# The row of means by way of DRAM instead of a TensorE transpose

## The chip, the cores and the metric

The kernel runs on one core of a Trainium2 chip, as one launch. The metric is device time in microseconds (us), the median of several executions. Times inside an execution come from one profiled execution and count from the start of its span. The engines are called by their names or as the profile abbreviates them: TensorE (PE, and PEld for its weight loads), VectorE (DVE), ScalarE (ACT), GpSimd (POOL) and SyncE (SP). An engine's name with a q (SPq, ACTq) stands for its instruction queue, where DMA issues are recorded.

## The reference

One transformer block on x of shape (4, 512, 512): four sequences of 512 tokens, 512 features, in float32. Cut to what is computed:

```python
def attn(x):                                  # x is layer-normalised
    q  = (x @ W_q.T).reshape(B, S, 16, 32)
    kv = (x @ W_kv.T).reshape(B, S, 16, 32)
    qf, kvf = fft(q), fft(kv)                 # over the 32 features of a head
    qf, kvf = qf / norm(qf), kvf / norm(kvf)
    kvf = cumsum(kvf, axis=1)                 # over the tokens of a sequence
    v = ifft(qf * kvf).real.reshape(B, S, D)
    return v @ W_o.T

def ffn(x):                                   # weights rounded to fp8 e4m3
    gate = silu((x @ q8(gate_w)) * gate_scale)
    up = (x @ q8(up_w)) * up_scale
    return ((gate * up) @ q8(down_w)) * down_scale

x = x + attn(layernorm(x))
x = x + ffn(layernorm(x))
```

The layer normalisation subtracts each token's mean over its features and divides by its deviation.

## The kernel before, in words

The work on attention is cut into 16 chunks of 128 tokens (four sequences of four chunks). A chunk is held twice: as x (tokens on the partitions, 128 x 512) and as xT (features on the partitions, four blocks of 128 x 128, tokens along the row). The Fourier transform is folded into the weights at the start, so one group of four matmuls makes the spectrum of a chunk (`spectrum`, L358: `pq`, with j = 1 for the keys and values and j = 0 for the queries).

The normalisation is split. The division by the deviation comes after the matmul, as a factor for each token. The subtraction of the mean comes before it, on xT. There the tokens lie along the row, so the means are needed as a row of 128 numbers that is the same on every partition. ScalarE makes the column of negated means, one number for each partition, in two operations (`x_mean`, L287 and L288, tile `less`). `x_row` (L344 to L346) then spreads the column over 128 columns by a broadcast access and lets TensorE transpose it into a PSUM tile `row`, whose every partition holds the row. `x_center` (L348 to L350) adds that row to the four blocks of xT on VectorE. `x_deviation` (L295 to L297) makes the reciprocal deviation on ScalarE and GpSimd.

The order of the instructions is written out by hand. After a prologue that treats chunks 0 to 2, a loop runs i from 3 to 15; its body is called a round here, and work on several chunks is interleaved in it. On each engine the instructions run in the order written. In a round:

- SyncE's queue issues the loads of xT and x for chunk i + 2, the reload of a finished chunk of the first sequence in some rounds (`load_y`, tile `ys`), the store of the attention's result for chunk i - 4 (`finish`, L466, `y_all`), loads of raw feed-forward weights (`load_unit`, L202, `rawf`), the store of the product of spectra for chunk i - 2 (`v_out`, L443, `qv_all`) and its reload in four pieces with another layout (`v_back`, L315, `zv`). In rounds 10 to 14 the same is done for the second normalisation of the first sequence (`y_out`, L491, `xn_all`; `y_back`, L315, `z`).
- TensorE runs the spectrum of chunk i (j = 1), the transpose of the means of chunk i + 1, the spectrum (j = 0), the running sum over tokens of chunk i - 1 (`running`, L413, `cum`) and the projection of chunk i - 3 (`project`, L457, `po`).
- VectorE scales by the norms (`kn`, `qn`, L382), adds the carried sum of the chunk before to the first row (L396), splits into high and low parts (`kl`, L404), finishes a chunk (L465), turns 32 x 32 blocks (`v_turn`, L320: `qvT` from `zv`; `t` from `z`), quantises the feed-forward weights, sums squares (L374), centres xT of chunk i + 1 (L350) and multiplies the spectra (L430, L431).
- ScalarE copies the high part (`kh`, L399), squares the spectra (L369), takes part in the quantisation (L217, L218), copies the last row of the running sum (`carry`, L420) and issues that row's move to partition 0 as a DMA from its own queue (L421, `end`, in twelve of the sixteen chunks), takes the mean of chunk i + 2 (L287, L288), and in rounds 9 to 12 the statistics of the second normalisation.

xT has three buffers, x seven. The PSUM tiles `row` share a tag of two buffers (`tp`) with some tiles outside the loop. The constant tile `tab` holds four 128 x 128 tables; the first (`fwd`, `tab[:, 0, :]`) is read only while the weights are folded in the prologue, the second is the identity that the transposes use.

A DMA tells its end by a semaphore. In the built program there are eight for the DMAs of both queues; they are taken in turn, and a DMA waits for the end of the one that had its semaphore before.

After the loop the feed-forward part runs 48 steps (four sequences of twelve blocks of 128 hidden features): gate and up projections (`gu`, L525), activation on ScalarE (L536), product on VectorE (L539), a split into high and low parts (L550, L552) and the down projection (`pd`, L572). Its first twelve steps overlap with the last chunks of the attention and with the rest of the quantisation.

Of the kernel before, what the change touches and what calls it, by code (L numbers as in the profile page):

```python
# [7 lines left out]
F32 = mybir.dt.float32  # L8
# [7 lines left out]
P = 128  # L16
# [19 lines left out]
def tile_fft_attention_then_fp8_ffn(  # L36
# [38 lines left out]
    nc = tc.nc  # L75
# [13 lines left out]
    dram = ctx.enter_context(tc.tile_pool(name="dram", bufs=1, space=bass.MemoryType.DRAM))  # L89
# [4 lines left out]
    N = len(chunks)  # L94


    tab = const.tile([P, 4, P], F32, name="tab")
# [16 lines left out]
    def big_tile(name, dtype=F32):  # L114
        return big.tile([P, KC, D], dtype, tag="big", name=name)

    raw = []
    for i, w in enumerate((w_kv, w_q, w_oT)):
        t = big_tile(f"raw{i}")
# [31 lines left out]
    wd = const.tile([P, MC, D], F32R, name="wd")  # L151
    y_all = dram.tile([B, TC, P, D], F32, name="y_all")
    xn_all = dram.tile([B, TC, P, D], F32, name="xn_all")
    qv_all = dram.tile([N, P, D], F32, name="qv_all")


# [37 lines left out]
    def load_unit(u):  # L194

        _, src, n, k = units[u]
        staged[u] = big_tile("rawf") if k == 0 else staged[u - 1]
        if src is down_w:
            rows = src[n * KC * P : (n + 1) * KC * P, :]
        else:  # L200
            rows = src[:, n * D : (n + 1) * D]
        nc.sync.dma_start(  # L202
            staged[u][:, k : k + QH, :],
            rows.rearrange("(k p) n -> p k n", p=P)[:, k : k + QH, :],
        )
# [63 lines left out]
    def next_parts(n, in_rounds=False):  # L269

        for f, u in parts[:n]:
            if f is quant_step:
                f(u, in_rounds)
                if in_rounds and u + 2 < U1 and u != 1:
                    wanted.append(u + 2)
            else:
                f(u)
            if f is quant_add and u + 1 < len(units):
                quant_abs(u + 1)
        del parts[:n]  # L280


    def mean(src, name):

        less = work.tile([P, 1], F32, tag="less", name=f"less_{name}", bufs=8)
        each = work.tile([P, D], F32, tag="each", name=f"each_{name}", bufs=1)
        nc.scalar.activation(each, src, AF.Identity, accum_out=less)  # L287
        nc.scalar.activation(less, less, AF.Copy, scale=-1.0 / D)  # L288
        return less
# [32 lines left out]
    def heads(t):  # L322
# [3 lines left out]
    st_x, lesses, rows, xns, pqs, sss, rns, qns, kns, carries, cums, qvs, zs, qvTs, pos = (  # L326
        {} for _ in range(15)
    )

    def nm(i):  # L330
        return "%d_%d" % chunks[i]

    def x_mean(i):
        st_x[i] = lesses[i] = mean(xt[i], nm(i))
# [9 lines left out]
    def x_row(i):  # L344
        rows[i] = ps.tile([P, KC, P], F32, tag="tp", name=f"row_{nm(i)}")
        nc.tensor.transpose(rows[i][:, 0, :], lesses[i].to_broadcast([P, P]), ident)  # L346

    def x_center(i):  # L348
        row = rows.pop(i)[:, 0:1, :].to_broadcast([P, KC, P])
        nc.vector.tensor_tensor(xTs[i], xTs[i], row, ALU.add)  # L350

    def spectrum(i, j):
        if j == 1:
            pqs[i] = {}
        pq = ps.tile([P, D], F32, tag="acc", name=f"pq{j}_{nm(i)}", bufs=4)
        w = (wq, wkv)[j]
        for k in range(KC):
            nc.tensor.matmul(  # L358
                pq, lhsT=xTs[i][:, k, :], rhs=w[:, k, :], start=k == 0, stop=k == KC - 1
            )  # L360
        pqs[i][j] = pq
# [5 lines left out]
    def squared(i, j):  # L367
        sq = sss[i, j] = work.tile([P, D], F32, tag="tmp", name=f"sq{j}_{nm(i)}")
        nc.scalar.activation(sq, pqs[i][j], AF.Square, scale=st_x[i][1])  # L369

    def summed(i, j):
        sq = sss[i, j]
        ss = work.tile([P, H], F32, tag=f"ss{j}", name=f"ss{j}_{nm(i)}")
        nc.vector.tensor_reduce(ss, heads(sq), AX.X, ALU.add)  # L374
        sss[i, j] = ss

    def norms(i, j):
        rns[i, j] = work.tile([P, H], F32, tag=f"rn{j}", name=f"rn{j}_{nm(i)}")
        nc.gpsimd.tensor_tensor(rns[i, j], sss.pop((i, j)), nhalf, ALU.pow)  # L379
# [11 lines left out]
    def k_scaled(i):  # L391
        kn = work.tile([P, D], F32, tag="kn", name=f"kn_{nm(i)}", bufs=1)
        scaled(i, 1, kn)
        if i in carries:
            row = carries.pop(i)
            nc.vector.tensor_tensor(kn[:1, :], kn[:1, :], row, ALU.add)  # L396
        kh = work.tile([P, D], F32R, tag="kh", name=f"kh_{nm(i)}", bufs=3)
        kl = work.tile([P, D], F32R, tag="kl", name=f"kl_{nm(i)}", bufs=3)
        nc.scalar.copy(kh, kn)  # L399
        kns[i] = (kn, kh, kl)  # L400

    def k_low(i):
        kn, kh, kl = kns[i]
        nc.vector.tensor_tensor(kl, kn, kh.bitcast(F32), ALU.subtract)  # L404

    def q_scaled(i):
        qns[i] = work.tile([P, D], F32, tag="qn", name=f"qn_{nm(i)}")
        scaled(i, 0, qns[i])

    def running(i, tag="b"):  # L410
        cum = ps.tile([P, D], F32, tag=tag, name=f"cum_{nm(i)}")
        for n, v in enumerate(kns[i][1:]):
            nc.tensor.matmul(cum, lhsT=tri_r, rhs=v, start=n == 0, stop=n == 1)  # L413
        cums[i] = cum
# [27 lines left out]
    def v_out(i):  # L442
        nc.sync.dma_start(qv_all[i], qvs.pop(i)[0])  # L443

    def v_back(i):
        zs[i] = work.tile([P, KC, P], F32, tag="z", name=f"zv_{nm(i)}")
        blocks(zs[i], qv_all[i])

    def v_turn(i):
        qvTs[i] = work.tile([P, KC, P], F32, tag="qvT", name=f"qvT_{nm(i)}", bufs=1)  # L450
        turned(qvTs[i], zs.pop(i))
# [19 lines left out]
    def load_y(b, chunks=None):  # L471
        if b not in ys:
            ys[b] = big_tile(f"ys_{b}")
        for c in range(TC) if chunks is None else chunks:
            nc.sync.dma_start(ys[b][:, c, :], y_all[b, c])

    def y_stats(b, c):
        st_y[b, c] = stats(ys[b][:, c, :], f"f{b}_{c}")
# [8 lines left out]
    def y_norm(b, c):  # L487
        xns["y", b, c] = normed(ys[b][:, c, :], st_y.pop((b, c)), f"f{b}_{c}")

    def y_out(b, c):  # L490
        nc.sync.dma_start(xn_all[b, c], xns.pop(("y", b, c)))  # L491

    def y_back(b, c):
        if b == 0:
            z = work.tile([P, KC, P], F32, tag="xn", name=f"z_{b}_{c}")
        else:
            z = work.tile([P, KC, P], F32, tag="x", name=f"z_{b}_{c}", bufs=XB)
        blocks(z, xn_all[b, c])
        xns["z", b, c] = z

    def y_turn(b, c):
        if c == 0:
            yhs[b] = big_tile(f"yh_{b}", F32R)
            yls[b] = big_tile(f"yl_{b}", F32R)
        z = xns.pop(("z", b, c))
        t = work.tile([P, KC, P], F32, tag="t", name=f"t_{b}_{c}", bufs=1)
        turned(t, z)
        s = slice(c * P, (c + 1) * P)
        hi, lo = yhs[b][:, :, s], yls[b][:, :, s]
        nc.scalar.copy(hi, t)  # L510
        return lo, t, hi.bitcast(F32)
# [76 lines left out]
    def at(f, i, *more):  # L588
        if 0 <= i < N:
            f(i, *more)  # L590
# [37 lines left out]
    squares(0, 1)  # L628
    norms(0, 1)
    x_row(1)  # L630
    x_center(1)
    spectrum(0, 0)
# [67 lines left out]
    for i in range(3, N):  # L700

        at(load_xT, i + 2)
        at(load_x, i + 2)
        if 0 <= i - (N - 9) < TC:
            load_y(0, [i - (N - 9)])
        spectrum(i, 1)
        k_scaled(i - 1)
        at(finish, i - 4)
        while wanted:
            load_unit(wanted.pop(0))  # L710
        v_out(i - 2)
        c = i - (N - 6)
        if 0 <= c < TC:
            y_norm(0, c)
            y_out(0, c)
        if 0 < c <= TC:
            y_back(0, c - 1)
        v_back(i - 2)
        k_low(i - 1)
        v_turn(i - 3)  # L720
        low = y_turn(0, c - 2) if 1 < c <= TC + 1 else None
        at(x_row, i + 1)
        squared(i, 1)
        at(x_deviation, i + 1)
        next_parts(given[i] // 3, True)
        q_scaled(i - 1)
        if low:
            nc.vector.tensor_tensor(*low, ALU.subtract)
        summed(i, 1)
        norms(i, 1)  # L730
        spectrum(i, 0)
        next_parts((given[i] + 1) // 3, True)
        running(i - 1)
        squared(i, 0)
        carry(i - 1)
        at(x_mean, i + 2)
        at(x_center, i + 1)
        products(i - 1)
        combined(i - 1)
        if 0 <= i - (N - 7) < TC:  # L740
            y_stats(0, i - (N - 7))
        summed(i, 0)
        norms(i, 0)
        next_parts((given[i] + 2) // 3, True)
        project(i - 3)
# [155 lines left out]
```

## Time and profile before

| | us |
|---|---|
| median of 3 runs | 459.96 |
| lowest, highest | 458.78, 460.82 |
| the profiled execution | 459.09 |
| its span | 457.3 |

What the span is made of, by the profile's chain of the work that ended last: the start with the folding of weights up to 16.7 us, the attention's chunks up to some 188 us, the feed-forward part to the end. In the loop a round takes 10.88 us (spectra of successive rounds begin at 114.94, 125.82, 136.71 and 147.58 us). The granted TensorE clock is full in every slice.

How to read the lines that follow: a line of a timeline has the start, the length, the engine, the line of the kernel, the operation, and what is written from what is read; in brackets stands how long the engine was idle before it, and which instruction ended that. A line of the waits has the engine and line that waited, what it waited for, the total, how often, and the longest. Median times from a DMA's issue to its landing, from the page:

| DMA | KB | us to landing |
|---|---|---|
| x, xT loads | 256 | 3.3, 3.2 |
| qv_all store, y_all store, xn_all store | 256 | 4.1, 2.7, 2.3 |
| zv reload, z reload (each of four) | 64 | 2.6, 2.7 |
| rawf load | 512 | 4.7 to 5.3 |
| end (carry), ScalarE's queue | 2 | 2.1 |

### The profile page before, as it was taken

Reading aid. Unit: us, or ns where it says so; the run is one execution under the profiler, and the core shown is the slowest. Engines: PE = TensorE matmul, PEld = TensorE weight load, DVE = VectorE, ACT = ScalarE, POOL = GpSimd, SP = SyncE. Lnnn points to the kernel's source line nnn. Section 1 sums busy time; section 2 is a strip of 40 time slices with the busy share of each in tenths; the row PEclk is TensorE's granted clock in tenths of the full one; section 3 lists DMA queues with packets and bytes.
Section 4 is the critical chain, followed back from the end, with each engine's and each line's share of the span. In section 5 each row is a group of like instructions: output and inputs, shape, how many; then the busy total and the mean of one; then the engine's idle time right before and its main releaser. Section 6 shows DMA issues by size and latency. Waiting matters only on the chain.

```text
span 457.3 us, 5096 instructions
## 1 busy us (share of the span) xinstructions
PE 451.2 (99%) x1692; PEld 309.0 (68%) x1692; DVE 283.1 (62%) x394; ACT 212.8 (47%) x430; POOL 186.1 (41%) x132
## 2 busy tenths in 40 slices
PE   8999999999999999999999999999999999999996
PEld 7544444444444445677888888888888888888885
DVE  1376998997999889797996432343533333522245
ACT  4467665555876632357834225433235432222230
POOL 0377898888797778500242230022401021400000
PEclk9999999999999999999999999999999999999999
DMA  8826366656687755752341050430141420200002
GB/s 299 300 77 191 101 162 161 184 150 185 196 212 201 178 134 151 216 149 96 92 93 23 0 185 23 93 69 0 48 139 38 101 46 1 92 1 0 0 1 92
DMA packets 91753, 51.22 MB, mean 112 GB/s; under 512 B 70608, under 2 KB 71248, under 8 KB 91728
## 3 DMA queue, kind: packets, MB, share of 16 engines
q1 hardware_dynamic: 91056, 50.75, 39.3%
q8 instruction: 13, 0.21, 0.2%
q10 hardware_dynamic: 672, 0.16, 0.2%
q14 instruction: 12, 0.10, 0.1%
HBM read 34.09 MB, written 16.78 MB: 111 GB/s over the span
## 4 chain that ended last, share of the span: by engine, by line
PE 90%; DVE 4%; DMA 2%; ACT 2%; issue 1%; DVEq 0%
PE gu L525 33%; PE pq L358 24%; PE pd L572 17%; PE po L457 12%; PE cum L413 2%; DMA raw<-in_w_q 1%; PE pw L162 1%; DVE qm L239 1%; PE pwo L175 1%; DVE f L539 1%; DMA tab<-in_tables 1%; ACT qm L218 1%; ACT qa L217 0%; DVE wu L252 0%; PE row L346 0%
## 5 line engine op out<-in xcount | busy, mean ns | idle before, releaser
L379 POOL TENSOR_TENSOR rn<-ss,nhalf 128x16 f32<-128x16 f32 x32 | 102.6, 3208 | 12.1 <-DVE ss L374 11.3
L539 DVE SCALAR_TENSOR_TENSOR f<-gu,gus,g 128x512 f32<-128x512 f32 x48 | 36.0, 750 | 99.9 <-PE gu L525 98.3
L525 PE MATMUL gu<-yh,wg 128*128 128x512 f32 x192 | 76.4, 398 | 0.0
L572 PE MATMUL pd<-wd,fh 128*128 128x512 f32 (+1 forms) x204 | 76.1, 376 | 0.0
L572 PE MATMUL pd<-wd,fl 128*128 128x512 f32 (+1 forms) x204 | 75.7, 377 | 0.0
L525 PE MATMUL gu<-yh,wu 128*128 128x512 f32 x192 | 74.8, 390 | 0.1
L525 PE MATMUL gu<-yl,wg 128*128 128x512 f32 x192 | 74.8, 390 | 0.0
L525 PE MATMUL gu<-yl,wu 128*128 128x512 f32 x192 | 74.7, 389 | 0.0
L550 ACT CAST fh<-f 128x512 fp32r<-128x512 f32 x48 | 29.8, 621 | 82.3 <-DVE f L539 82.3
L536 ACT ACTIVATE g<-gu,gus 128x512 f32<-128x512 f32 x48 | 33.0, 688 | 55.6 <-PE gu L525 55.3
L358 PE MATMUL pq<-wq,xT 128*128 128x512 f32 x128 | 57.6, 592 | 0.0
L358 PE MATMUL pq<-wkv,xT 128*128 128x512 f32 x128 | 57.5, 592 | 0.0
L457 PE MATMUL po<-wo,qvT 128*128 128x512 f32 x128 | 57.5, 592 | 0.0
L552 DVE TENSOR_TENSOR fl<-f,fh 128x512 fp32r<-128x512 f32 x48 | 35.8, 745 | 27.6 <-ACT fh L550 27.5
L358 PEld LDWEIGHTS pq<-wkv,xT 128*128 128x128 f32 x128 | 24.2, 190 | 30.1 <-issue 28.7
L572 PEld LDWEIGHTS pd<-wd,fl 128*128 128x128 f32 x204 | 38.4, 188 | 7.3
L572 PEld LDWEIGHTS pd<-wd,fh 128*128 128x128 f32 x204 | 38.3, 188 | 7.3
L297 POOL TENSOR_TENSOR dev_f<-dev_f,nhalf 128x1 f32<-128x1 f32 x16 | 10.7, 670 | 77.3 <-ACT dev_f L296 77.3
L358 PEld LDWEIGHTS pq<-wq,xT 128*128 128x128 f32 x128 | 23.2, 190 | 27.4 <-issue 27.0
L525 PEld LDWEIGHTS gu<-yh,wg 128*128 128x128 f32 x192 | 36.1, 188 | 8.1 <-issue 0.7
L525 PEld LDWEIGHTS gu<-yl,wg 128*128 128x128 f32 x192 | 36.1, 188 | 8.1 <-issue 1.0
L525 PEld LDWEIGHTS gu<-yh,wu 128*128 128x128 f32 x192 | 36.0, 188 | 7.9 <-DVE f L539 0.5
(91 smaller groups left out, 589.5 us busy)
## 6 DMA issues: line engine op xcount, KB each, us to landing
x<-in_x SPq DMA_DIRECT2D x16, 256.0 KB, 3.3
xT<-in_xT SPq DMA_DIRECT2D x16, 256.0 KB, 3.2
qv_all<-qv SPq DMA_DIRECT2D x16, 256.0 KB, 4.1
zv<-qv_all SPq DMA_DIRECT2D x64, 64.0 KB, 2.6
y_all<-x SPq DMA_DIRECT2D x16, 256.0 KB, 2.7
ys<-y_all SPq DMA_DIRECT2D x16, 256.0 KB, 3.5
xn_all<-xn_f SPq DMA_DIRECT2D x16, 256.0 KB, 2.3
z<-xn_all SPq DMA_DIRECT2D x64, 64.0 KB, 2.7
```

Source lines behind the costliest of these rows:

```text
L162: nc.tensor.matmul(pw[:, j * P : (j + 1) * P], lhsT=r[:, j, i * P : (i + 1) * P], rhs=fwd, start=True, stop=True,)
L297: nc.gpsimd.tensor_tensor(rstd, rstd, nhalf[:, 0:1], ALU.pow)
L358: nc.tensor.matmul(pq, lhsT=xTs[i][:, k, :], rhs=w[:, k, :], start=k == 0, stop=k == KC - 1)
L379: nc.gpsimd.tensor_tensor(rns[i, j], sss.pop((i, j)), nhalf, ALU.pow)
L413: nc.tensor.matmul(cum, lhsT=tri_r, rhs=v, start=n == 0, stop=n == 1)
L457: nc.tensor.matmul(po, lhsT=qvT[:, k, :], rhs=wo[:, k, :], start=k == 0, stop=k == KC - 1)
L525: nc.tensor.matmul(p, lhsT=w[:, k, m * P : (m + 1) * P], rhs=v[:, k, :], start=k == 0 and v is yhs[b], stop=k == KC - 1 and v is yls[b],)
L536: nc.scalar.activation(g, pgu[0], AF.Silu, scale=gus[:, 0, m : m + 1])
L539: nc.vector.scalar_tensor_tensor(f, pgu[1], gus[:, 1, m : m + 1], g, ALU.mult, ALU.mult)
L550: nc.scalar.copy(fh, f)
L552: nc.vector.tensor_tensor(fl, f, fh.bitcast(F32), ALU.subtract)
L572: nc.tensor.matmul(p, lhsT=v[:, c * P : (c + 1) * P], rhs=wd[:, m, s], start=m == 0 and v is fused[n][0], stop=m == MC - 1 and v is fused[ ...
```

## The change

From chunk 5 on (the sixth) the row of means is no longer made by TensorE. After ScalarE has made the column, it issues a DMA from its own queue that stores it to DRAM (`mean_out`, 128 pieces of 4 bytes, in round i for chunk i + 2). In the next round SyncE's queue issues a DMA that reads the 128 numbers back as a row onto every partition (`mean_back`, 128 rows of 512 bytes), after the load of x and, where there is one, of `ys`. Its target is the first table of `tab`, which is free by then; it is one buffer for all chunks, so a read waits until the centring of the chunk before has used it. `x_center` reads its row from there. Chunk 4's transpose stays, in round 3.

```diff
     xn_all = dram.tile([B, TC, P, D], F32, name="xn_all")
+    means = dram.tile([N, P, 1], F32, name="means")
     qv_all = dram.tile([N, P, D], F32, name="qv_all")
...
+    def mean_out(i):
+        nc.scalar.dma_start(means[i], lesses[i])
+
+    def mean_back(i):
+        rows[i] = tab[:, 0:1, :]
+        nc.sync.dma_start(
+            rows[i][:, 0, :], means[i].rearrange("t o -> (o t)").partition_broadcast(P)
+        )
...
         if 0 <= i - (N - 9) < TC:
             load_y(0, [i - (N - 9)])
+        if 4 < i + 1 < N:
+            mean_back(i + 1)
         spectrum(i, 1)
...
         low = y_turn(0, c - 2) if 1 < c <= TC + 1 else None
-        at(x_row, i + 1)
+        if i == 3:
+            x_row(4)
         squared(i, 1)
...
         carry(i - 1)
-        at(x_mean, i + 2)
+        if i + 2 < N:
+            x_mean(i + 2)
+            mean_out(i + 2)
         at(x_center, i + 1)
```

## The prediction

> **What bounds the kernel now.** I read the page first: the busy shares, then the shares of the chain that ended last.
>
> ```profile
> PE 451.2 (99%) x1692; PEld 309.0 (68%) x1692; DVE 283.1 (62%) x394; ACT 212.8 (47%) x430; POOL 186.1 (41%) x132
> ...
> PE 90%; DVE 4%; DMA 2%; ACT 2%; issue 1%; DVEq 0%
> PE gu L525 33%; PE pq L358 24%; PE pd L572 17%; PE po L457 12%; PE cum L413 2%; DMA raw<-in_w_q 1%; PE pw L162 1%; DVE qm L239 1%; PE pwo L175 1%; DVE f L539 1%; DMA tab<-in_tables 1%; ACT qm L218 1%; ACT qa L217 0%; DVE wu L252 0%; PE row L346 0%
> ```
>
> TensorE is the bound from end to end, and the row of means (L346) is on its chain. The chain in order of time gives one round of the attention loop (start, length, what):
>
> ```profile
> 125.82 3.43 PE pq L358 x8
> 129.26 0.11 PE row L346
> 129.37 3.44 PE pq L358 x8
> 132.80 0.47 PE cum L413 x2
> 133.27 3.44 PE po L457 x8
> 136.71 3.43 PE pq L358 x8
> ```
>
> A round is 136.71 - 125.82 = 10.89 us without a gap, and the transpose is 0.11 of it. So there is a gain only while VectorE, ScalarE and the loads keep their lead over TensorE. Busy time by stretch, one round each (i = 10, 11, 12; after the span's length come PE, PEld, DVE, ACT, POOL, then clock, DMA share, GB/s):
>
> ```profile
> 114.94:125.82 10.88, 10.88 (x29) 5.00 (x28) 10.63 (x17) 8.77 (x21) 8.62 (x5) 1.00 0.67 200
> 125.82:136.71 10.89, 10.89 (x29) 5.00 (x28) 10.64 (x16) 8.59 (x21) 9.90 (x7) 1.00 0.86 217
> 136.71:147.58 10.87, 10.87 (x28) 4.99 (x28) 10.46 (x16) 6.70 (x19) 8.51 (x7) 1.00 0.76 209
> ```
>
> VectorE is nearly as full as TensorE. The reader is to see that a delay of VectorE is not absorbed by idle time there; it is absorbed only by the lead. The lead is small: centring (L350) ends at 145.9 in round 12 and 157.1 in round 13, and its readers start at 147.58 and 158.47, so 1.7 and 1.35 us.
>
> **What is removed.** Eleven transposes (chunks 5 to 15). By the chain 11 x 0.11 = 1.2 us, all on the path. Their record says more:
>
> ```profile
> L346 PE MATMUL row<-tab,less x16: 270/272/273, 9.3 to 161.7; 128*128 128x128 f32 x16
> ```
>
> That 272 ns overlaps its neighbours; 3.43 + 0.11 + 3.44 + 0.47 + 3.44 fills the round, so 0.11 is what it displaces. If 0.27 were displaced, the gain would be 11 x 0.27 = 3.0 us.
>
> [...]
>
> Does 1.2 us survive the feed-forward part? There ScalarE and VectorE lie on the chain from 213 to 240 us. That stretch starts with ScalarE waiting 1.53 us for TensorE (gate activation at 213.05), so it moves forward with TensorE. I carry all of it.
>
> **What is added on ScalarE.** Eleven stores of 128 x 4 bytes, each behind its mean. The nearest row is the carry's issue:
>
> ```profile
> L421 ACTq DMA_DIRECT2D end<-end x12: 504/505/610, 26.7 to 178.0; - x12
> ```
>
> After it ScalarE stands idle for 0.58 us until its next operation, so 11 x 0.58 = 6.4 us of ScalarE. Behind the store stand the sums of the feed-forward part and then the copy kh, which already waits for VectorE, 1.2 to 3.5 us in all rounds but two: in round 6 the idle time is split (1.01 and 0.73 us), and in round 12 kh at 151.41 follows without a pause. There 0.58 us goes to kl, which VectorE waits for, and with it to the centring of chunk 14: 1.35 us of lead less 0.58. Cost with cover 0; without the cover of rounds 9 to 12, 4 x 0.58 = 2.3 us.
>
> **What is added on SyncE.** Eleven reads of 64 KB (128 rows of 512 bytes), some 0.43 us of issue each like x (L111), between the load of x and y_all. SyncE has a pause there; its waits in total, times, longest:
>
> ```profile
> SPq L315 <- DMA qv_all<-qv: 39.6, 15, 5.1
> SPq L466 <- DVE x L465: 35.1, 12, 8.6
> ...
> SPq L315 <- DMA end<-end: 1.9, 1, 1.9
> ```
>
> L466 (y_all) waits for VectorE anyway, so the issue is free, except in rounds 12 and 13 where SyncE runs without a pause (from 139.93 to 143.18): there 2 x 0.43 us are added to the store and reload of qv.
>
> **The round trip.** No row shows a 4-byte-per-partition store. Bounds: 1.6 us (fastest carry) and 5.6 us (longest store of qv_all or xn_all, behind a 512 KB load). I take 2.3, the median of xn_all, nearest in direction; the carry, nearest in size, has 2.1. For the read: 2.3 us (fastest zv) to 6.6 us (longest x); I take 3.3, the median of x, behind which it stands. A broadcast read isn't slow by itself: dsc was read in a stretch of 386 GB/s. Then in round 5 the mean is ready at 59.95, the store starts at 60.0 and has landed at 62.3, the read lands at 65.6, and the centring was at 67.77: 2.2 us to spare. In round 8 98.8 against 100.46, in round 11 131.9 against 134.16, in round 12 144.3 against 145.21. So the trip is hidden, with 0.9 us at its tightest. Waiting for the centring to release the one shared row costs nothing: that centring ran a round earlier.
>
> [...]
>
> **Centring** reads its row from SBUF instead of PSUM. A subtraction with all operands in SBUF (kl, L404) took 692 ns against 680: 11 x 0.012 = 0.1 us on VectorE; at the slowest record of kl (723) 0.5 us. Off the path.
>
> **What is moved: the waits for the completion semaphores.** In the built program all DMAs take eight semaphores in turn, in one order over both queues, and each waits for the transfer that had its semaphore before. Twenty-two more DMAs shift that order. In round 11 of before, the second zv waits for the carry's landing (the 1.9 us above):
>
> ```profile
> 135.49 4.35 SPq L315 DMA_DIRECT2D zv<-qv_all  x4
> 139.93 0.57 SPq L106 DMA_DIRECT2D xT<-in_xT  x1
> 140.54 0.43 SPq L111 DMA_DIRECT2D x<-in_x  x1
> 141.07 0.38 SPq L466 DMA_DIRECT2D y_all<-x  x1
> ```
>
> After the change it is the fourth z that waits for that carry, so four zv stand behind it, not three, and the second zv waits for the new store of round 11. ScalarE runs half a microsecond earlier by then (five transposes saved when it last waited for TensorE, at 107.6), so the carry lands at 137.9 - 0.5 = 137.4 and the store at 136.6 - 0.5 + 2.3 = 138.4, just ahead of the second zv (137.4 + 2 x 0.65 = 138.7). The last zv starts at 137.4 + 4 x 0.65 = 140.0, not 139.2. It lands at 142.6 (2.6 us) and the turn (L320, at 141.81 before) ends at about 143.3. TensorE, 9 x 0.11 = 1.0 us ahead, wants it at 144.15 - 1.0 = 143.15. So a wait of 0.2 us in round 12, and, with the uncovered store and SyncE's 0.43 us, about 0.3 us more in round 13. I take 0.5 us; bounds 0 and 1.5 (0.8 us of shift, 0.43 + 0.58 late besides, against lead already spent).
>
> **Sum**, against the profiled execution's 459.09 us (span 457.3): -1.2 + 0.5 = -0.7, so 458.4. The median shown, 459.96, is 0.87 above that execution; on the median the forecast is 459.3.
>
> **Rivals.**
> 1. Hidden throughout: no waits, -1.2 us, 458.8. For it: TensorE has no gap in any round. Against: the shifted waits in rounds 11 to 13.
> 2. ScalarE and VectorE become the bound. From kh to kh they took 11.1 us in rounds 10 to 12 (117.81, 128.94, 140.04), above a round. If the four stores lie in that loop, 4 x 0.58 = 2.3 us against a lead of 1.7 - 1.0 = 0.7: TensorE waits 1.6 us, net +0.4, 460.4. Against: the store is issued while VectorE does other work of the loop.
> 3. Slower: the store lands late. In round 11 the second zv waits for it. At 5.6 us it lands at 136.1 + 5.6 = 141.7, the last zv starts at 143.0 and lands at 145.6, the turn ends at 146.3 against 143.15: TensorE waits 3.1 us. In rounds 12 and 13 the read then waits 1 us too, and y_all, qv and zv behind it: some 1.5 us more. Net -1.2 + 3.1 + 1.5 = +3.4, 463.4. It decides from a landing of 2.6 us up (138.7 - 136.1), and is over half a per cent from some 4.7 us. For it: DMA is busy 0.86 of round 11, and the carry's landings reach 4.0 us. Against: at 138 to 139 us no byte moves.
> 4. The transpose displaces its whole 272 ns: -3.0 + 0.5, 457.5. Against: the chain.
>
> **How the numbers follow.** Forecast 0.48, rival 1 0.13, rival 2 0.10, rival 3 0.23, rival 4 0.06. The likeliest's own range is 458.6 to 460.5 (waits of 0 to 1.5 us, and the spread of the three runs). A measurement of this kernel can't tell less than 0.5% (2.3 us) from no change, so the forecast and rivals 1 and 2 are "no change"; rival 4 is faster at its edge, rival 3 slower: 0.06, 0.70, 0.24 with its tail of the forecast. The range leaves out rival 4 and the upper half of rival 3: 458.2 to 463.6.
>
> **What would show it.** TensorE's rounds of 10.77 us up to round 11 (right), or still 10.88 (rival 2 or 3). The store's landing near 2.3 us; the read's landing before the centring, with no VectorE wait on DMA at L361. In round 11 the second zv released by the carry's or the store's landing, the turn of round 12 near 143, and a first gap of TensorE in front of the projection of round 12. I am wrong if TensorE shows gaps in the early rounds, or if the saving is gone by 213 us.

## The result, and the profile after

| | before | after |
|---|---|---|
| median, us | 460.05 (4 runs) | 517.86 (4 runs) |
| lowest, highest | 458.78, 460.82 | 514.40, 519.69 |
| the profiled execution's span | 457.3 | 516.5 |

The ratio is 1.126, with a 95% interval of 1.123 to 1.128. The kernel became 58 us slower; 459.3 was predicted, with a range up to 463.6. In the listing of after, the lines of the rounds stand some eleven further down: L321 is the turn `qvT`, L316 the reload `zv`, L454 the store `qv_all`, L468 the projection `po`. The new store is L351, the new read L355, and the centring L361.

The page of after answers first: busy time, then the shares of the chain that ended last.

```profile
PE 469.5 (91%) x1681; PEld 313.5 (61%) x1681; DVE 283.3 (55%) x394; ACT 213.3 (41%) x430; POOL 186.2 (36%) x132
...
PE 53%; DMA 25%; DVE 6%; issue 5%; ACT 4%; SPq 4%; POOL 3%; DVEq 0%; POOLq 0%; ACTq 0%
```

TensorE had 90% of the chain before and has 53% now; DMA went from 2% to 25%. The 59.2 us of span split in two. TensorE's idle time went from 457.3 - 451.2 = 6.1 to 516.5 - 469.5 = 47.0 us, 40.9 more. And it is busy 18.3 us longer with eleven instructions fewer, so it ran slower in places. Most of that is in the projection, whose line in the pages of before and after (out of and into which tiles, busy us and mean ns, idle time before) went from 57.5 to 73.1 us, 15.6 more:

```profile
L457 PE MATMUL po<-wo,qvT 128*128 128x512 f32 x128 | 57.5, 592 | 0.0
...
L468 PE MATMUL po<-wo,qvT 128*128 128x512 f32 x128 | 73.1, 724 | 38.2 <-DVE qvT L321 38.1
```

The waits of after name who is late (engine and line, what it waited for, total, times, longest):

```profile
PE po L468 <- DVE qvT L321: 38.1, 10, 6.0
...
DVE qvT L321 <- DMA zv<-qv_all: 54.5, 11, 7.6
...
SPq L316 <- DMA qv_all<-qv: 65.8, 15, 10.6
...
SPq L355 <- DMA means<-less: 25.0, 4, 10.4
```

Read from the top: the projection waits for the turned product, the turn for the reload `zv`, and the reload is issued late because the store `qv_all` is late (39.6 us of such waits before, 65.8 now). None of these three handles a mean. The wait that belongs to the change, of the read for its store, is the fourth line. It is 25.0 us on SyncE in four rounds, and what is behind it in SyncE's order starts later with it (behind the longest, of 10.4 us, the read starts at 56.92, `y_all` at 57.35 and `qv_all` at 57.82); whether it makes the loss is what experiment 3 asks. On TensorE the late row itself shows in two gaps of 2.3 us together, in front of the spectra at 62.05 and 113.08.

The page's list of DMAs (KB of each, median us from issue to landing):

```profile
qv_all<-qv SPq DMA_DIRECT2D x16, 256.0 KB, 5.6
...
y_all<-x SPq DMA_DIRECT2D x16, 256.0 KB, 4.2
...
means<-less ACTq DMA_DIRECT2D x11, 0.5 KB, 9.3
```

Half a KB takes 9.3 us, longer than any other group on the list (7.1 at the least, 11.5 at the most). The 256 KB stores that ran beside it got slower too: `qv_all` from 4.1 to 5.6, `y_all` from 2.7 to 4.2.

How a large store ends late beside a small one shows in one round's timeline of after:

```profile
57.82 0.38 SPq L454 DMA_DIRECT2D qv_all<-qv  x1
...
59.41 0.33 ACTq L351 DMA_DIRECT2D means<-less  x1
68.93 2.61 SPq L316 DMA_DIRECT2D zv<-qv_all  x4
73.79 0.71 DVE L321 STREAM_TRANSPOSE qvT<-zv 128x512 f32<-128x512 f32 x1 [7.05 <-DMA zv<-qv_all]
74.55 5.33 PE L468 MATMUL po<-wo,qvT 128*128 128x512 f32 x8 [4.91 <-DVE qvT L321]
```

The 256 KB store, issued at 57.82, lands at 68.9, after 11.1 us. The store of the means, issued at 59.41, lands 9.7 us later, at 69.1. For most of that time the DMA engines have nothing to do. These are their busy share, in tenths, and what they moved, from 57 to 77 us in slices of 0.5 us:

```profile
DMA  0000014796200000000000000025575799999933
GB/s 0 0 0 0 6 45 156 281 381 246 66 0 0 0 0 0 0 0 0 0 0 0 0 0 0 0 44 92 86 124 86 121 116 328 389 308 334 169 17 65
```

Bytes move from 59 to 62.5 us; then all is still until 70. The slices up to there add up to 1181 GB/s x 0.5 us = 590 kB. The three transfers that SyncE issued from 56.92 to 57.82 (a read of a row, `y_all`, `qv_all`) make 64 + 256 + 256 = 576 KB, which is 590 kB. So by this sum `qv_all` wasn't slowed for want of bandwidth: its data were through by 62.5, and its end was told 6.4 us later. Two more rounds have the late end and the still engines (`qv_all` from 108.80, after 10.2 us, with the engines all but still from 114.3; and from 139.22, after 10.6, with the engines still from 143.9 to 149.4), each with a store of means issued 1.6 us behind it; where the next store of means was issued 5.7 and 3.1 us behind it, it landed after 5.0 us (92.49) and 3.9 (124.31). It is not the only delay: the `qv_all` issued at 74.16, right behind a load of 512 KB, took 7.4 us with no store of means beside it but one issued 0.4 us before its end.

In the three rounds `qv_all` ends 0.2, 1.0 and 0.3 us ahead of the store of means beside it. What the rows show is the coincidence of the ends and the idle engines; what ties the one end to the other they don't show.

The slower TensorE comes behind the gap. The stretch after that gap (start and end; length, busy time of PE, PEld, DVE, ACT, POOL, then granted clock, DMA share, GB/s):

```profile
74.50:78.00 3.50, 3.45 (x4) 1.51 (x5) 3.50 (x4) 2.27 (x3) 1.00 (x1) 0.52 0.90 220
```

The granted clock is 0.52 in these 3.5 us (1.00 in the next four), and the projection, 3.60 us elsewhere, takes 5.33.

### The profile page after: what moved, and what is told of

The parts are those of the page before. It is cut to its first block, busy times and chain, and to the rows that moved or that the text cites. A ratio compares the mean times of both kernels' runs of the same rounds, so it can differ in the third digit from the quotient of the medians.

```text
span 516.5 us, 5106 instructions
## 1 busy us (share of the span) xinstructions
PE 469.5 (91%) x1681; PEld 313.5 (61%) x1681; DVE 283.3 (55%) x394; ACT 213.3 (41%) x430; POOL 186.2 (36%) x132
## 4 chain that ended last, share of the span: by engine, by line
PE 53%; DMA 25%; DVE 6%; issue 5%; ACT 4%; SPq 4%; POOL 3%; DVEq 0%; POOLq 0%; ACTq 0%
PE gu L536 30%; PE pd L583 15%; DMA qv_all<-qv 9%; DMA means<-less 4%; DMA zv<-qv_all 4%; PE pq L369 3%; DMA xT<-in_xT 3%; SPq L316 3%; POOL rn L390 2%; DMA xn_all<-xn_f 2%; PE po L468 2%; DMA x<-in_x 1%; ACT qm L219 1%; PE pkv L163 1%; PE pw L163 1%
## 5 line engine op out<-in xcount | busy, mean ns | idle before, releaser
L468 PE MATMUL po<-wo,qvT 128*128 128x512 f32 x128 | 73.1, 724 | 38.2 <-DVE qvT L321 38.1
L468 PEld LDWEIGHTS po<-wo,qvT 128*128 128x128 f32 x128 | 28.8, 234 | 74.9 <-DVE qvT L321 42.9
L369 PE MATMUL pq<-wq,xT 128*128 128x512 f32 x128 | 57.5, 592 | 0.0
L321 DVE STREAM_TRANSPOSE qvT<-zv 128x512 f32<-128x512 f32 x16 | 11.3, 708 | 54.5 <-DMA zv<-qv_all 54.5
```

The source lines that it names most:

```text
L321: nc.vector.transpose(t.rearrange("p k n -> p (k n)"), z.rearrange("p k n -> p (k n)"))
L369: nc.tensor.matmul(pq, lhsT=xTs[i][:, k, :], rhs=w[:, k, :], start=k == 0, stop=k == KC - 1)
L468: nc.tensor.matmul(po, lhsT=qvT[:, k, :], rhs=wo[:, k, :], start=k == 0, stop=k == KC - 1)
```

## The experiments

The theory after this reading: the store of means lands late, and until it has landed it holds up the ends of other transfers. The rivals: the read waits for the store (in short, the dependence is at fault); one more transfer in each round is at fault, however soon it lands (SyncE's time, the shifted turn of the semaphores); the read of 64 KB is at fault. The kernel before ran beside all of them, with medians of 459.74 to 459.76.

**1. The store alone.** The kernel before, transposes kept, with the eleven stores; nothing reads them.

```diff
+    def mean_out(i):
+        nc.scalar.dma_start(means[i], lesses[i])
...
-        at(x_mean, i + 2)
+        if i + 2 < N:
+            x_mean(i + 2)
+            mean_out(i + 2)
```

> The kernel before, with its transposes, plus the eleven stores of the means to DRAM, which nothing reads. Wait theory (the loss is SyncE's queue standing at the read until the store has landed): no instruction waits for the store but by a shared semaphore, so the time is that of before plus the uncovered issues, 460 to 462 us; the store lands after some 9 us here too, and qv_all lands after 4.1 us as before. Hold-up theory (while the 4-byte pieces are being written, the ends of other transfers are held back until they have landed, whoever issued them): qv_all, zv, x and xT that are in flight beside a store land up to 10 us after their issue, VectorE waits for zv at the turn, and half of the loss or more is back: 480 us or more. Semaphore theory (the shifted order of the eight semaphores costs it): between, 465 to 475 us, with SyncE's waits on the store and not on qv_all.

Measured: 512.37, ratio 1.113 (1.108 to 1.117). The stores landed after 8.9 us (median), and SyncE's waits for `qv_all` were 71.9 us. Four stores of `qv_all` (issued at 83.58, 105.08, 137.78 and 152.91) landed after 9.8 to 16.2 us, each 0.2 to 0.9 us ahead of a store of means. Nothing reads the means here; SyncE stood only in the turn of the semaphores for a store of means, 13.7 us in three waits. So 512.37 - 459.74 = 52.6 of the 58 us come without the dependence.

**2. The read alone.** The changed kernel without the store. The read takes a row of a constant table, so the centring adds that row in place of the means.

```diff
-            rows[i][:, 0, :], means[i].rearrange("t o -> (o t)").partition_broadcast(P)
+            rows[i][:, 0, :], tables[i, 0, :].partition_broadcast(P)
...
             x_mean(i + 2)
-            mean_out(i + 2)
```

> The change without its store: the read back fetches a row of a constant table instead, so the centring uses the wrong numbers; all else as in the change, the transposes gone. Wait theory and hold-up theory alike: the store is the whole cause, so 459 to 461 us, the read landing after some 3.3 us and hidden. If the read itself or its place in SyncE's queue costs something (read theory), 465 us or more with VectorE waiting at the centring.

Measured: 464.88, ratio 1.010 (1.007 to 1.013). Its projections, one for each round, in the timeline of this kernel:

```profile
122.80 3.60 PE L468 MATMUL po<-wo,qvT 128*128 128x512 f32 x8
133.77 3.70 PE L468 MATMUL po<-wo,qvT 128*128 128x512 f32 x8
147.29 5.40 PE L468 MATMUL po<-wo,qvT 128*128 128x512 f32 x8 [2.27 <-DVE qvT L321]
159.86 3.60 PE L468 MATMUL po<-wo,qvT 128*128 128x512 f32 x8
```

Up to 122.80 the rounds take 10.76 us (the projection before stands at 112.04), against 10.88 before. Then come 10.97, 13.52 and 12.57 us: the reads cost nothing early and some 5 us late.

**3. Store and read, unlinked.** The changed kernel with the constant read of experiment 2, so that nothing waits for the store.

```diff
-            rows[i][:, 0, :], means[i].rearrange("t o -> (o t)").partition_broadcast(P)
+            rows[i][:, 0, :], tables[i, 0, :].partition_broadcast(P)
```

> The change with its store and its read, but the read fetches a row of a constant table, so it doesn't wait for the store (the centring uses the wrong numbers). Wait theory: the wait at the head of SyncE's queue is gone, so 459 to 463 us. Hold-up theory: SyncE no longer stands at the read, but qv_all and zv still land late, so most of the loss stays: 485 to 515 us. The difference to the change is what the wait alone costs.

Measured: 521.27, ratio 1.133 (1.124 to 1.141). The dependence is gone and the time is that of the change or more. The read's wait for its data is not the cause. SyncE still stands for stores of means, which nothing reads here, so by the turn of the semaphores. These are lines of its waits:

```profile
SPq L454 <- DMA means<-less: 6.1, 1, 6.1
...
SPq L355 <- DMA means<-less: 5.5, 1, 5.5
...
SPq L106 <- DMA means<-less: 4.6, 1, 4.6
...
SPq L203 <- DMA means<-less: 4.0, 1, 4.0
...
SPq L316 <- DMA means<-less: 1.3, 1, 1.3
```

That is 21.5 us, beside 73.5 us of waits for `qv_all`. The late stores cost in two ways here, then: other transfers end late beside them, and whoever has their semaphore next waits.

**4. Forms of a store.** Single stores from ScalarE's queue in the quiet last part of the feed-forward stage, two of each form, added to the kernel before; nothing reads them.

> The kernel before plus fourteen single stores from ScalarE's queue in the feed-forward part, where the DMA engines are nearly idle, two each of seven forms: 128 pieces of 4 bytes side by side (pa), the same 512 bytes apart (pb), 32 pieces of 4 bytes (pc), 128 pieces of 64 bytes (pe), 128 of 512 bytes (pf), 16 of 4 bytes (pg), and 128 of 4 bytes into SBUF (ph). If the pieces' number sets the landing (each engine writes its eight one after the other), pa and pb land after some 9 us, pc after 3 to 4, pg after 2 to 2.5. If neighbours in one stretch of memory get in each other's way, pb lands after 2 to 3 us and pa after 9. If the size below 512 bytes sets it, pe lands after 9 us too and pf after 2. If it is DRAM, ph lands after 2 us. If it was only the load on the DMA engines in the attention part, all land after 2 to 3 us here.

Landings (KB, median us) by the list of DMAs. `pa` is the form of the change, 128 pieces of 4 B side by side; `pb` the same 512 B apart; `pc` 32 pieces and `pg` 16 pieces of 4 B side by side; `pe` 128 pieces of 64 B and `pf` 128 of 512 B; `ph` 128 pieces of 4 B into SBUF, one for each partition:

```profile
pf<-dsc ACTq DMA_DIRECT2D x2, 64.0 KB, 1.5
pa<-eps ACTq DMA_DIRECT2D x2, 0.5 KB, 8.8
pb<-eps ACTq DMA_DIRECT2D x2, 0.5 KB, 1.5
pc<-eps ACTq DMA_DIRECT2D x2, 0.1 KB, 3.8
pe<-dsc ACTq DMA_DIRECT2D x2, 8.0 KB, 1.4
pg<-eps ACTq DMA_DIRECT2D x2, 0.1 KB, 1.3
ph<-eps ACTq DMA_DIRECT2D x2, 0.5 KB, 2.6
```

The two stores of `pa` took 10.2 us (issued at 267.8, beside other transfers) and 7.5 us (at 347.5). This is the stretch of the second and one of `pb`, with DMA share and GB/s at the end:

```profile
281.90:284.00 2.10, 2.10 (x11) 1.69 (x10) 0.24 (x1) 1.79 (x5) 0.55 (x1) 1.00 0.04 0
...
347.50:355.00 7.50, 7.50 (x34) 6.04 (x33) 1.90 (x3) 3.80 (x10) 1.10 (x2) 1.00 0.09 31
```

On all but idle DMA engines the same 128 pieces of the same 4 B take 7.5 us side by side and 1.4 us (the median of the two is 1.5) apart. So neither load, nor the size of a piece, nor their number alone made the landing late here, but where they fall. (The whole kernel took 466.79 us in its one run, because the feed-forward groups of TensorE took 3.73 us for 3.63 from before the first of these stores on. Why stays open; the next run of this kind took 459.23.)

**5. The same store, spread.** Experiment 3 with each piece 512 B from the next: same count, same bytes, same queue, same turn of the semaphores.

```diff
-    means = dram.tile([N, P, 1], F32, name="means")
+    means = dram.tile([N, P, P], F32, name="means")
...
-        nc.scalar.dma_start(means[i], lesses[i])
+        nc.scalar.dma_start(means[i][:, 0:1], lesses[i])
```

> The kernel with the store and the read unlinked (521.3 us), but each of the 128 four-byte pieces goes to a place of its own, 512 B from the next, a form that landed after 1.4 to 1.7 us beside 7.5 to 10.2 for pieces side by side. The same number of transfers, pieces and bytes, the same queue, the same turn of the semaphores; the read takes a row of a constant table, so the centring is done with that row in place of the means. If the late end of the store holds up the ends of the other transfers: the store lands in 1.4 to 2.5 us, the v store's landings fall back from 8.6 to about 4 us in the rounds, and the time is that of the kernel with the read alone, 464 to 466. If a store more in each round is the cause, however soon it lands (its place in the turn of the semaphores, its 128 pieces): 515 or more.

Measured: 463.20, ratio 1.008 (1.005 to 1.010). The DMA list, and the wait of the reload, of this kernel:

```profile
means<-less ACTq DMA_DIRECT2D x11, 0.5 KB, 2.3
```

```profile
SPq L316 <- DMA qv_all<-qv: 41.2, 14, 6.0
```

The store lands after 2.3 us, SyncE's waits for `qv_all` fall from 73.5 us in experiment 3 to 41.2 (39.6 before), and 521.27 - 463.20 = 58 us come back. Only where the pieces fall was changed, and with it the landing; no wait of SyncE for a store of means is left. This settles the store in its slow form, with its late landing, as the cause; what remains is no more than the read alone costs. How the 58 us split between ends held up and semaphores held, experiments 3 and 5 don't say, since both go together.

**6. The change with a store in four pieces.** All of the change, linked: VectorE turns the column in blocks of 32 x 32, and the store takes the first row of each block, four pieces of 128 B.

```diff
+    def mean_turned(i):
+        nc.vector.transpose(inv[:, (i % 2) * 32 : (i % 2) * 32 + 32], lesses[i].to_broadcast([P, 32]))
+
     def mean_out(i):
-        nc.scalar.dma_start(means[i], lesses[i])
+        turn = inv[::32, (i % 2) * 32 : (i % 2) * 32 + 32]
+        nc.scalar.dma_start(means[i].rearrange("(a b) o -> a (b o)", b=32), turn)
...
         products(i - 1)
+        if i + 2 < N:
+            mean_turned(i + 2)
         combined(i - 1)
...
         norms(i, 0)
+        if i + 2 < N:
+            mean_out(i + 2)
```

> The whole change, linked, with a row that is stored in four pieces of 128 B: VectorE turns the column of means in 32x32 blocks, and the store takes partitions 0, 32, 64 and 96 of the turned block. If the pieces of 4 B side by side are the cause: the store lands within 2 us, the read waits for nothing, and the time is that of the kernel with the read alone plus eleven short turns on VectorE, 464.5 to 466.5. If what is read back only just after it was written costs anything of itself: over 470. Faster than before (under 459.0) under neither.

Measured: 467.52, ratio 1.017 (1.015 to 1.020). Fifty of the 58 us are gone with the means still on their way through DRAM, but it is 1.0 us above the expected range. No landing of this store was recorded. It now starts later in the round, and the read waits for it in three rounds, as this line of its waits shows (`tab<-` and `<-tab`: the turned block lies in `tab`):

```profile
SPq L359 <- DMA means<-tab: 10.2, 3, 5.7
```

**7. No row at all.** Transposes gone, nothing stored or read; the centring adds a row of a constant table that is in SBUF from the start.

```diff
     def mean_back(i):
         rows[i] = tab[:, 0:1, :]
-        nc.sync.dma_start(
-            rows[i][:, 0, :], means[i].rearrange("t o -> (o t)").partition_broadcast(P)
-        )
...
             x_mean(i + 2)
-            mean_out(i + 2)
```

> The eleven transposes are gone and nothing takes their place: the centring adds a row of a constant table that lies in SBUF since the start (so the centring is done with that row in place of the means). This is all that the change could have gained. By the rounds of the kernel with the read alone (10.77 us where before took 10.88), 11 x 0.11 = 1.2 us less: 458.5 beside 459.7. If each transpose displaces the 272 ns of its own span: 456.7. If the gain of a round is given back at the end of the rounds: 459.7.

Measured: 458.93, ratio 0.9984 (0.9971 to 0.9997), 0.8 us less. This is the most that the change could have won. Its timeline at the end of the rounds:

```profile
164.38 3.60 PE L464 MATMUL po<-wo,qvT 128*128 128x512 f32 x8
...
179.04 0.47 PE L532 MATMUL gu<-yh,wg 128*128 128x512 f32 x1 [0.31 <-DVE cross L438]
...
183.61 0.50 PE L420 MATMUL cum<-kl,tri_r 128*128 128x512 f32 x1 [0.23 <-DVE kl L411]
183.95 3.59 PE L464 MATMUL po<-wo,qvT 128*128 128x512 f32 x8
```

And before:

```profile
165.75 3.59 PE L457 MATMUL po<-wo,qvT 128*128 128x512 f32 x8
...
184.37 3.59 PE L457 MATMUL po<-wo,qvT 128*128 128x512 f32 x8
```

The projection at 164.38 stood at 165.75 before, a lead of 1.37 us. At 179.04 and 183.61 TensorE waits for VectorE, and the projection at 183.95, at 184.37 before, has a lead of 0.42 us left. The profiled span is 456.9, 0.4 below before.

**8. The read from ScalarE's queue.** Experiment 2 with the eleven reads issued by ScalarE at the same place.

```diff
-        nc.sync.dma_start(
+        nc.scalar.dma_start(
             rows[i][:, 0, :], tables[i, 0, :].partition_broadcast(P)
```

> The kernel with the read alone (464.9), with the eleven reads issued by ScalarE's queue at the same place of the program, so that the turn of the semaphores stays as it was there and only SyncE is relieved of 11 x 0.43 us. If its 5 us are SyncE's, which runs without a pause in rounds 10 to 14: 458.5 to 460.5. If they come from the shifted turn of the semaphores: 464 to 465.5. If a transfer that begins in the middle of the others takes their bandwidth: 464 too, but with longer landings and no wait of SyncE for a carry's transfer. As in the kernel with the read alone, the centring adds a row of a constant table.

Measured: 462.06, ratio 1.005 (1.003 to 1.007), between the theories. The waits say why it can't decide: in the order of ScalarE the read now stands behind the work of a round, and SyncE waits for semaphores that it holds, here the store of `qv_all` (and once, 3.2 us, that of `y_all`):

```profile
SPq L454 <- DMA tab<-in_tables: 3.5, 2, 2.7
```

**9. The shift of the semaphores, without a read.** Experiment 7 with the spread stores of experiment 5, so one transfer more in each of eleven rounds, none on SyncE.

```diff
+    def mean_out(i):
+        nc.scalar.dma_start(means[i][:, 0:1], lesses[i])
...
             x_mean(i + 2)
+            mean_out(i + 2)
```

> The kernel without transposes and without a row (458.9), with the eleven stores in the form that lands soon (pieces 512 B apart); nothing reads them, and the centring adds the row of a constant table. So the semaphores' turn is shifted by one transfer in each of eleven rounds, but SyncE issues nothing more. If the shifted turn by itself costs the 5 us that the read alone lost at the end of the rounds: 463 to 465. If SyncE's own time for the reads, or the semaphores that end late only with a 64 KB transfer on them, cost it: 458.5 to 460.

Measured: 460.73, ratio 1.002 (1.000 to 1.003), between the theories again. Its rounds keep 10.75 us up to 143.31, and the next two take 11.35 and 11.20 us. One more soon-landing transfer in each of eleven rounds, its issue on ScalarE included, costs 460.73 - 458.93 = 1.8 us, of the 464.88 - 458.93 = 6.0 us that the read alone costs over no row.

**10. The reads of rounds 4 to 8 only.** Experiment 2, with the later chunks centred by the row left in SBUF.

```diff
-        nc.sync.dma_start(
-            rows[i][:, 0, :], tables[i, 0, :].partition_broadcast(P)
-        )
+        if i < 10:
+            nc.sync.dma_start(
+                rows[i][:, 0, :], tables[i, 0, :].partition_broadcast(P)
+            )
```

> The kernel with the read alone (464.9), but only the five reads of the chunks from the sixth to the tenth are made, in rounds 4 to 8; the later chunks are centred with the row of a constant table that the last of them left. If a read costs nothing where SyncE has pauses and its price lies in rounds 10 to 14: 458.5 to 459.6, near the 458.9 of the kernel without any. If a read costs something wherever it stands (about 0.5 us each by 464.9 - 458.9 over eleven): 461.5 to 462.

Measured: 459.15, ratio 0.9985 (0.9966 to 1.0005). Five reads cost 0.2 us together, which the spread of the runs doesn't tell from nothing; the other six cost the rest, 464.88 - 459.15 = 5.7 us. The price of the reads lies in the late rounds.

**11. More forms of a store**, as in experiment 4.

> Stores from ScalarE's queue into DRAM in the quiet part of the feed-forward stage, two of each, beside the kernel before; nothing reads them. Landings, if pieces that share one short stretch of DRAM with others are slow and each stretch is 64 B: 128 pieces of 4 B side by side 7 to 10 us; 16 B apart 7 to 10 or a little less; 32 B apart some 3 to 6; 64 B apart under 2; side by side but handed out so that successive pieces lie 128 B apart still 7 to 10; 64 pieces side by side 4 to 6; 4 pieces of 128 B under 2. If only successive pieces that touch are slow: 16 B apart and the permuted form land under 2 us. If the number of bytes of each piece is what counts, all forms of 4 B pieces would be slow, which the 512 B apart of the earlier look speaks against.

Here `pa` is the form of the change again, `pc` 128 pieces of 4 B that lie 32 B apart (64 B apart took 2.0 us), `pf` 128 pieces side by side whose successive pieces lie 128 B apart, and `pg` 64 pieces side by side:

```profile
pa<-eps ACTq DMA_DIRECT2D x2, 0.5 KB, 9.0
...
pc<-eps ACTq DMA_DIRECT2D x2, 0.5 KB, 1.8
...
pf<-eps ACTq DMA_DIRECT2D x2, 0.5 KB, 6.8
pg<-eps ACTq DMA_DIRECT2D x2, 0.2 KB, 7.6
```

The two of `pa` took 10.5 and 7.4 us, the second again where the DMA engines had little to do. Pieces 32 B apart landed soon, after 1.8 us, which neither theory of this run had down to (64 B stretches were expected to be slow at 32 B, too). Handing neighbours out in another order helped little (6.8). No landing was recorded for 16 B apart, nor for four pieces of 128 B.

## Why the prediction was wrong, point by point

**The step that failed is the round trip:** "No row shows a 4-byte-per-partition store. Bounds: 1.6 us ... and 5.6 us ... I take 2.3". It landed after 9.3 us, outside both bounds. The nearest rows in direction and in size were stores whose pieces are long, or a single row; none had short neighbours, and that is what counted (experiments 4 and 11: 128 pieces of 4 B took 7.4 to 10.5 us side by side, 1.5 to 2.0 from 32 B apart on). The length of a piece by itself doesn't show in these landings: 128 pieces of 512 B landed after 1.5 us, of 64 B after 1.4, and of 4 B, 512 B apart, after 1.5.

**The larger part of the miss is an effect that the sum had no term for.** The late landing was to cost only those who wait for the row, or for its semaphore (rival 3: from 2.6 us up, in rounds 11 to 13, 463.4). Rival 3 had the right first step, a late store, with a chance of 0.23, but not its reach: by its arithmetic a landing of 9.3 us gives a stall of some 7 us once, not 58. What the late store did was to hold up the ends of 256 KB stores from round 4 on, and the next holders of its semaphores, in a loop of store, reload, turn and projection in which TensorE then waited 38.1 us for the turn. Experiment 3 shows that the wait for the row is not needed for it, experiment 5 that the store in the form that landed after 2.3 us removes it: 58 us. The prediction's own sign of being wrong, gaps of TensorE in the early rounds, is there from 62.05 us on. By what mechanism the small stores held the ends of the large ones stays open.

**The gaps cost twice.** 40.9 us are TensorE's idle time, and 18.3 us its longer busy time, 15.6 of them in the projections, which stand behind the gaps; behind the gap shown above the granted clock was 0.52. The prediction priced waits alone.

**0.11 us for a transpose was right.** Rounds of 10.75 to 10.77 us in experiments 2, 7 and 10 against 10.88; rival 4 (0.27) falls.

**"Does 1.2 us survive the feed-forward part?"** was answered yes from the stretch behind 213 us, and should have been asked at 179 us: there the first steps of that part wait for VectorE, and 1.37 us of lead become 0.42 (experiment 7). The chain of before had it: from 180.14 to 184.03 us it ran over VectorE and ScalarE, and ended with

```profile
183.29 0.70 DVE kl L404
184.03 0.50 PE cum L413
```

so VectorE set the pace there, and TensorE lost most of its lead at it. The median gain without any row is 0.8 us.

**SyncE's reads** were to cost 2 x 0.43 us inside a term of 0.5 us, with a bound of 1.5; alone they took back the gain and 5 us more (464.88). The place was right, rounds 11 to 13 in the trace and free before that (experiment 10), the size was not. The shift of the semaphores, with eleven issues on ScalarE, is 1.8 us (experiment 9), against the bound of 1.5. How the other 4 us split between SyncE's issue time and semaphores held by the reads is open, since experiment 8 changed both.

**The rest.** "A broadcast read isn't slow by itself" holds roughly: 3.8 us in experiment 2, 3.3 taken. The centring from SBUF took 693 ns against 680 in `x_center` before, as taken. The ScalarE issue was shorter than taken (0.34 us against 0.50, and at 141.22 us ScalarE goes on 0.41 us after the mean, against 0.58), and rival 2 shows nowhere: with the spread store and its issues the time isn't above that of the read alone.

## What to carry to other kernels

A column of single numbers, stored to DRAM so that the pieces lie side by side, ended late here (9.3 us), and large stores of another queue ended late with it (up to 11.1 us): look at the landing of the smallest transfer when large ones on another queue get slow, and at whether the DMA engines are idle while they are waited for. Spread the pieces (32 B apart was enough for a single store, 1.8 us, and 512 B in the kernel, 2.3 us), or turn the column first so that each piece is long (467.52 us in place of 517.86 with four pieces of 128 B). And before taking an instruction of 0.11 us off the bounding engine, remove it without a replacement: here that showed a ceiling of 0.8 us in 460, too little to pay for the six reads of the late rounds, which cost 5.7 us.

## What the runs showed of the hardware that had not been expected

- The landing of a store of 4 B pieces side by side grew with their number up to 64: 16 took 1.3 us, 32 took 3.8, 64 took 7.6, two stores of each. 128 took 7.4 and 7.5 where the DMA engines had little else to do, no more than 64, and 10.2 and 10.5 beside other transfers. The same 128 pieces took 1.8 us when 32 B apart. So the distance from which on neighbours landed soon here is 32 B or less; why closer ones were slow was not shown.
- A transfer whose bytes were through by 62.5 us, by the sum of what was moved, was told as ended at 68.9, together with a later, smaller one of another queue.
- After gaps of little over 2 us TensorE ran slower in some cases: a projection of 3.60 us took 5.40 after a wait of 2.27 us (experiment 2, granted clock 0.68 in the 5.41 us from its start), 5.34 after one of 2.42 (after, at 139.39 us, 0.69) and 5.40 after one of 2.13 (experiment 5), but 3.70 after one of 1.77 (experiment 6), of 2.12 and 2.65 (after, at 108.90 and 205.32 us, granted clock 1.00) and even of 3.10 (experiment 1). The length of the wait alone didn't decide it.
